# One fused GNN and transformer kernel: edge lists read before the last row tiles are turned, projections split around the counting stage, pair sums of weights formed before a move

## The chip, the cores and the metric

The kernel runs on one core of a Trainium2 chip. The metric is the device time of one execution in microseconds (us), as the median of several. The core has five engines with a queue each: TensorE (PE in the profile; its weight loads are PEld), VectorE (DVE), ScalarE (ACT), GpSimd (POOL) and SyncE (SP, which here only issues DMAs). They run beside each other and wait for each other through semaphores.

## The reference

`x` is 1250 x 768 in fp32. There are 41250 edges (`src`, `dst`), sorted by `dst`, with a loop at each node.

```
y   = layernorm(x)
h   = gat(y, W1, a_src1, a_dst1, b1);  h = relu(h)
x   = x + gat(h, W2, a_src2, a_dst2, b2)

gat(y):  h = y @ W;  e = leaky_relu((h @ a_src)[src] + (h @ a_dst)[dst])
         w = exp(e - max over the edges of a dst)
         out[dst] = sum(w * h[src]) / sum(w) + b

z   = layernorm(x)
z1  = z + attention(layernorm(z))          # 12 heads of 64, 1250 tokens
z2  = z1 + moe(layernorm(z1))              # 8 experts, the best 2 of each token
out = x + z2
```

The reference works in fp32 throughout.

## The kernel before

Nodes go in ten row tiles of 125 (T = 125, NT = 10), features in six chunks of 128 (DC = 6). An fp32 matmul shows as two passes in the profile.

**Rows and edge lists (from L219).** The edge key `dst * 1250 + src` is written to a DRAM list. For each of five blocks of two row tiles (NU = 5) an indirect DMA gathers a row of the list, `first_edges` counts with it where the block's edges begin, and a second indirect DMA gathers windows of 128 keys into `win` (L307). Meanwhile the row tiles are loaded and normalised: `spread(t)` takes mean and variance on VectorE and the root on ScalarE, `normal(t)` scales the row on ScalarE, and `columns(t)` turns the tile on PE into `xnT` (L146), with two evictions on ScalarE (L278). `project` multiplies a row tile by `gW1` (L209: 12 matmuls, 24 passes) and evicts it to `h` (L212). A `manual_schedule` block fixes the order of PE, VectorE and POOL here, as written; ScalarE's order is the planner's, except that `keep_in_program_order` puts an instruction behind the one that was written before it on its engine. The planner is the library's: it orders by its own costs the instructions whose order the text does not fix.

Behind the tiles the list entries are cleaned on VectorE (L358 to L371), a matmul `psum` (L373) counts the valid ones, `good` and `turns` (L375, L377) say whether the lists hold every edge, five transposes turn `win` into `pl` (L385) and ScalarE copies them to `lt` (L386). `lt` and `jf` lie in a pool, `onehot`, that takes the space of the row tiles.

**Counts (L399 to L412).** The counts are a 1250 x 1250 matrix of how often an edge occurs, `cnt`. In 25 groups VectorE builds a one-hot `ohp` by comparing with `lane` (L405), and for each five groups one `ohj` by comparing with `upto` (L402); both lie in `onehot` too. PE multiplies them, 25 matmuls a group (L409), and ScalarE casts the result into `cnt` (L411). `lane` and `upto` are filled by POOL's iota (L255, L337). A loop of `turns` iterations (L418), which the given lists run zero times, follows; at its end every engine waits until all that was issued before it is done. Instructions written behind it are ordered by themselves.

**First graph layer.** Loops are added to `cnt` (L438). VectorE multiplies `gW1` by the two attention vectors (`attention_vector`, L187), PE multiplies the result by `xnT` (`attention_terms`, L199, three chunks) and turns the terms to columns (L478). VectorE forms the maximum over the neighbours (L489). `rest_of_first` then projects the tiles that are left, `range(EARLY, NT)` with EARLY = 3: seven of ten. ScalarE and VectorE make the weight tiles (L517 to L522, ten for each of three parts, twelve buffers), and PE aggregates (L529). The second layer does the same with `gW2`.

**Attention (from L612).** Products of the weights run by a scheme with seven instead of eight block products (`seven`), for which POOL forms sums and differences of blocks. Of the weights: `left_sums` (L639 to L642), once for each of six pairs of heads, in `queries_keys(p)`, whose loads of `wqk` SP issues (L701). Of the rows: `t2`, `t3`. These are moved by POOL (L877, L878) into `kept`, in the space of the value weights `wv`, once PE has read `wv` for the last time. A unit is a pair of heads and a third of the queries: PE makes `scores` (L752), ScalarE copies them out of PSUM (L756; two buffers), VectorE keeps the maximum (L762) and subtracts it (L783), ScalarE takes exponentials (L784), POOL adds them up (L789, `acc`) and PE makes `values` (L797). PE's order is written out by hand in the loop over units; the products of the next pair (L684) go between.

In the code before, `queries_keys(1)` begins at the first round of that loop, behind the two moves:

```
            kept = wpool.tile([P, DC, D], F32, tag="w", name="kept")...
            ys = right(*parts(kept, NH, 2))
            nc.gpsimd.tensor_copy(ys[5], t2)
            nc.gpsimd.tensor_copy(ys[6], t3)
```

The projection, the experts and the routing behind it are not touched.

Of the kernel before, what the change touches and what calls it, by code (L numbers as in the profile page):

```python
# [27 lines left out]
def gnn_ffn_kernel(  # L28
# [137 lines left out]
    with tc.tile_pool(name="cnt", bufs=1) as cpool:  # L166
# [49 lines left out]
            nc.vector.memset(h[:, :, D:D + 1], 1.0)  # L216
            return h

        EARLY = 3  # L219
        with tc.tile_pool(name="edge", bufs=1) as ep, \  # L220
                tc.tile_pool(name="epc", bufs=2, space=PSUM) as epc, \
                tc.tile_pool(name="gpt0", bufs=2, space=PSUM) as gpt, \
# [11 lines left out]
            for i, (eng, a) in enumerate(((nc.sync, dst), (nc.scalar, src))):  # L234
# [16 lines left out]
            nc.gpsimd.iota(nodes, pattern=[[N, N]], base=0, channel_multiplier=0,  # L251
                           allow_small_or_imprecise_dtypes=True)

            lane = ep.tile([P, P, PG], BF16, name="lane")
            nc.gpsimd.iota(lane, pattern=[[1, P], [0, PG]], base=0, channel_multiplier=0,  # L255
                           allow_small_or_imprecise_dtypes=True)
            upto = ep.tile([P, 2 * NT, 5 * PG], BF16, name="upto")


# [21 lines left out]
            with tc.tile_pool(name="early", bufs=1) as xp:  # L281
# [46 lines left out]
                with tc.manual_schedule(engines=fixed):  # L328
                    pk = find_rows()
                    spread(0)  # L330
                    nc.vector.tensor_scalar(row, pk[:T, :NU], -1.0, None, ALU.add)
                    nc.vector.tensor_scalar(edges, pk[:T, :NU], -1.0, float(EC), ALU.add, ALU.mult)
                    for u in range(NU):
                        nc.gpsimd.indirect_dma_start(
                            out=krows[u], out_offset=None, in_=rows,
                            in_offset=bass.IndirectOffsetOnAxis(ap=row[:, u:u + 1], axis=0))
                    nc.gpsimd.iota(upto, pattern=[[1, 2 * NT], [0, 5 * PG]], base=1, channel_multiplier=0,  # L337
                                   allow_small_or_imprecise_dtypes=True)
                    for t in range(1, 4):
                        spread(t)  # L340
                        normal(t - 1)
                        columns(t - 1)
                    normal(3)
                    columns(3)

                    for t in range(4, NT):
                        if t < 4 + NU:
                            first_edges(t - 4)
                        spread(t)
                        if t > 4:  # L350
                            normal(t - 1)
                        if t % 2 == 0:
                            project(xT, gw, h, gpo, [t // 2 - 2])
                        if t > 4:
                            columns(t - 1)
                    normal(NT - 1)
                    columns(NT - 1)
                    nc.vector.tensor_tensor(win, win, pair[:, :, None].to_broadcast([T, NU, SL]), ALU.subtract)  # L358

            op = edge.enter_context(tc.tile_pool(name="onehot", bufs=2))  # L360
            reps = [every_partition(a, op, "rep", nc.sync) for a in (ga_src1, ga_dst1)]

            wf = win.rearrange("p u s -> p (u s)")
            ge = ep.tile([T, NU * SL], F32, name="ge")
            nc.vector.tensor_scalar(ge, wf, 0.0, None, ALU.is_ge)
            found = ep.tile([T, 1], F32, name="found")
            nc.vector.scalar_tensor_tensor(ge, wf, 2.0 * N, ge, op0=ALU.is_lt, op1=ALU.mult,
                                           accum_out=found)
            FAR = 1048576.0
            nc.vector.scalar_tensor_tensor(wf, wf, FAR, ge, op0=ALU.add, op1=ALU.mult)  # L370
            nc.vector.tensor_scalar(wf, wf, -FAR, None, ALU.add)  # L371
            pf = gpt.tile([P, 4, P], F32, tag="tr", name="psum")
            nc.tensor.matmul(pf[:, 0, 0:1], ones[:T, :P], found, start=True, stop=True)  # L373
            good = ep.tile([P, 1], F32, name="good")
            nc.vector.tensor_scalar(good, pf[:, 0, 0:1], float(E), None, ALU.is_equal)  # L375
            turns = ep.tile([1, 1], I32, name="turns")
            nc.vector.tensor_scalar(turns, good[0:1], -float(EC // EB), float(EC // EB), ALU.mult, ALU.add)  # L377


            lt = op.tile([P, NP], F32, name="lt", bufs=1)  # L380
            for u0 in range(0, NU, 4):
                n = min(4, NU - u0)
                pt = gpt.tile([P, 4, P], F32, tag="tr", name="pl")
                for u in range(u0, u0 + n):
                    nc.tensor.transpose(pt[:, u - u0, :T], win[:, u, :], ident[:T, :T])  # L385
                nc.scalar.copy(lt[:, u0 * T:(u0 + n) * T].rearrange("p (u q) -> p u q", q=T), pt[:, :n, :T])  # L386

            jf = op.tile([P, NP], F32, name="jf", bufs=1)
            half = (T - 1) // 2
            nc.vector.tensor_scalar(jf, lt, -float(half), 1.0 / T, ALU.add, ALU.mult)  # L390
            nc.vector.tensor_scalar(jf, jf, 12582912.0, -12582912.0, ALU.add, ALU.add)
# [44 lines left out]
            for t in range(NT):  # L436
                d = cnt[:, t, t * T:(t + 1) * T]
                nc.vector.tensor_tensor(d, d, ident[:T, :T], ALU.add)  # L438
            for i, a in enumerate(reps):
                attention_vector(0, i, gw, a, op, "scr")  # L440
            attention_terms(xT, gpt)
# [2 lines left out]
        with tc.tile_pool(name="gwork", bufs=2) as gp, \  # L444
# [166 lines left out]
    with tc.tile_pool(name="att", bufs=2, reuse_waits="tile") as ap, \  # L611
# [126 lines left out]
        class Unit:  # L738
# [42 lines left out]
            def weights(self, j):  # L781
                w, s = self.w, self.s[j]
                nc.vector.tensor_tensor(s[:, :, :w], s[:, :, :w], self.mb[:T, :, :w], ALU.subtract)  # L783
                nc.scalar.activation(s[:, :, :w], s[:, :, :w], AF.Exp, scale=HD ** -0.5)  # L784
                if j == 1:
                    self.acc = ap.tile([T, 2, CW], F32, tag="acc", name="acc", bufs=1)
                if 0 < j < self.ns:
                    prev = self.s[0] if j == 1 else self.acc
                    nc.gpsimd.tensor_tensor(self.acc[:, :, :w], prev[:, :, :w], s[:, :, :w], ALU.add)  # L789

            def values(self, j):
                w, s = self.w, self.s[j]
# [41 lines left out]
        with tc.tile_pool(name="tsum", bufs=1, reuse_waits="tile") as tp, \  # L834
# [42 lines left out]
            nc.gpsimd.tensor_copy(ys[5], t2)  # L877
            nc.gpsimd.tensor_copy(ys[6], t3)  # L878
        apm = ring.enter_context(tc.tile_pool(name="apm", bufs=1, space=PSUM, reuse_waits="tile"))
        apa = ring.enter_context(tc.tile_pool(name="apa", bufs=1, space=PSUM, reuse_waits="tile"))  # L880
        sx = ring.enter_context(tc.tile_pool(name="sx", bufs=1, reuse_waits="tile"))
        rings[NT:] = [sx] * (RING - NT)
        units = [(p, k) for p in range(DC) for k in range(NCK)]
        steps = last = None
        waiting = []
        for n, (p, k) in enumerate(units):
            if k == 0:
                steps = None
                if p + 1 < DC:
                    steps = queries_keys(p + 1, ys, False)  # L890
# [414 lines left out]
```

## Time and profile before

| | |
|---|---|
| median of 3 executions | 1499.6 us (1499.52 to 1505.01) |
| profiled execution | 1501.22 us |
| its span on the core | 1499.4 us |
| PE busy | 1407.0 us, 94% |
| VectorE, ScalarE, POOL busy | 813.4, 572.1, 490.1 us |
| HBM | 88 GB/s over the span |

Times in the views count from the span's start. A row of the timeline is: start, duration, engine, line, operation, output <- inputs, shape, count, and in brackets the idle time of the engine before it with what ended it. L12 is line 12 of the kernel before. In the 40 slices a digit is the busy share in tenths, and PEclk is the clock that TensorE was granted, in tenths.

### The profile page before, as it was taken

What the parts mean: (1) busy time and instruction counts of PE and PEld (TensorE: products, weight loads), DVE (VectorE), ACT (ScalarE), POOL (GpSimd) and SP (SyncE); (2) the same over time, 40 slices, a digit from 0 to 9 for tenths busy, and PEclk for the clock granted to TensorE, in tenths of its full rate; (3) what the DMA queues carried; (4) which work ended last, traced back from release to release, by engine and by line L of the source; (5) the groups of instructions that cost most, each with busy time, mean ns of one, the idle gap of its engine ahead of it and who ended that gap; (6) DMA issues with size and microseconds to landing.
All of it is one profiled execution on the core that took longest, in us unless ns stands there. A gap on an engine that the chain in (4) does not pass through costs nothing. (4 is left out here: it accounts for less than half of the span.)

```text
span 1499.4 us, 16427 instructions
## 1 busy us (share of the span) xinstructions
PE 1407.0 (94%) x6032; PEld 791.8 (53%) x6032; DVE 813.4 (54%) x1390; ACT 572.1 (38%) x920; POOL 490.1 (33%) x345
## 2 busy tenths in 40 slices
PE   5787999999999999989999999999989999899997
PEld 3584655555555556544444444444433666565654
DVE  5598545535025754356767767767767655111111
ACT  4220603205115621135656656656656223221211
POOL 5000000000000065025776867776767222222222
PEclk9757999999999999999999999999999999999999
DMA  7000020000021114990101000000001734665653
GB/s 210 22 1 11 11 74 0 1 7 26 0 87 59 52 50 157 378 363 1 33 7 28 12 8 27 13 28 7 12 19 64 238 114 146 228 227 171 225 188 121
DMA packets 55581, 128.46 MB, mean 86 GB/s; under 512 B 10797, under 2 KB 29585, under 8 KB 55498
## 3 DMA queue, kind: packets, MB, share of 16 engines
q1 hardware_dynamic: 38846, 61.18, 12.7%
q0 software_dynamic: 11968, 56.21, 10.3%
q10 hardware_dynamic: 4684, 9.99, 2.2%
q8 instruction: 48, 0.79, 0.2%
q14 instruction: 35, 0.29, 0.1%
HBM read 74.17 MB, written 57.66 MB: 88 GB/s over the span
## 5 line engine op out<-in xcount | busy, mean ns | idle before, releaser
L789 POOL TENSOR_TENSOR acc<-acc,sT 125x834 f32<-125x834 f32 (+1 forms) x139 | 273.0, 1964 | 10.7
L529 PE MATMUL pagg<-h,wt 125*125 125x385 f32 (+1 forms) x800 | 263.5, 486 | 0.4 <-DVE wt L522 0.4
L529 PEld LDWEIGHTS pagg<-h,wt 125*125 125x125 f32 x800 | 147.0, 187 | 104.6 <-DVE wt L522 3.5
L756 ACT COPY sT<-st 125x834 f32<-125x834 f32 (+1 forms) x180 | 151.3, 849 | 126.0 <-PE st L752 119.9
L783 DVE TENSOR_TENSOR sT<-sT,mb 125x834 f32<-125x834 f32 (+1 forms) x180 | 174.9, 1011 | 31.4 <-PE mb L778 31.4
L762 DVE TENSOR_TENSOR most<-most,st 125x834 f32<-125x834 f32 (+1 forms) x144 | 146.8, 1020 | 59.2 <-ACT sT L756 55.7
L784 ACT ACTIVATE sT<-sT 125x834 f32<-125x834 f32 (+1 forms) x180 | 158.4, 901 | 46.7 <-DVE sT L783 46.1
L752 PE MATMUL st<-qk 64*125 64x417 f32 (+1 forms) x720 | 163.9, 555 | 11.8 <-DVE most L762 8.3
L639 POOL TENSOR_TENSOR aT<-wv 128x1152 f32<-128x1152 f32 x1 | 2.6, 2615 | 490.0 <-DVE wt L522 490.0
L797 PE MATMUL pav<-sT,v 125*64 125x417 f32 (+1 forms) x720 | 151.0, 532 | 5.5 <-ACT sT L784 3.7
L752 PEld LDWEIGHTS st<-qk 64*125 64x125 f32 x720 | 57.0, 184 | 102.4 <-DVE most L762 51.4
L797 PEld LDWEIGHTS pav<-sT,v 125*64 125x64 f32 x720 | 42.7, 136 | 96.2 <-issue 56.1
L1039 PE MATMUL poe<-we,hT 128*128 128x384 f32 x264 | 89.8, 486 | 0.0
L1006 PE MATMUL phe<-xT,we 128*128 128x384 f32 (+1 forms) x288 | 86.6, 460 | 0.0
L1068 PE MATMUL po<-wp,aT 128*125 128x384 f32 x240 | 86.6, 497 | 0.0
L209 PE MATMUL ph<-gw,xnT 128*125 128x384 f32 x240 | 81.9, 501 | 3.4 <-DMA gw<-in_L_gnn_W_dram 3.4
L789 POOL TENSOR_TENSOR acc<-sT 125x834 f32<-125x834 f32 (+1 forms) x18 | 35.4, 1968 | 142.5 <-ACT sT L784 142.5
L533 DVE RECIPROCAL rz<-pagg 125x1 f32<-125x1 f32 x20 | 3.3, 166 | 141.0 <-PE pagg L529 141.0
L209 PE MATMUL ph<-gw,x1T 128*125 128x384 f32 x240 | 78.8, 489 | 0.0
L1008 ACT ACTIVATE hT<-phe 128x384 f32<-128x384 f32 (+2 forms) x30 | 13.1, 437 | 155.5 <-PE phe L1006 155.5
L1006 PEld LDWEIGHTS phe<-xT,we 128*128 128x128 f32 x288 | 52.1, 190 | 33.6
L1043 DVE SCALAR_TENSOR_TENSOR sofar<-poe,weight,sofar 128x768 f32<-128x768 f32 x23 | 23.4, 1018 | 82.5 <-PE poe L1039 82.5
(286 smaller groups left out, 1945.3 us busy)
## 6 DMA issues: line engine op xcount, KB each, us to landing
xd<-aT POOLq DMA_DIRECT2D x8, 3855.0 KB, 49.0
we<-in_L_ffn_W_dram SPq DMA_DIRECT2D x16, 1152.0 KB
xr<-xd SPq DMA_DIRECT2D x25, 385.5 KB
gw<-in_L_gnn_W_dram SPq DMA_DIRECT2D x2, 2304.0 KB
wqk<-in_L_ffn_Wqkv_dram SPq DMA_DIRECT2D x12, 384.0 KB
xres<-in_x_dram SPq DMA_DIRECT2D x10, 375.0 KB
xsd<-xres ACTq DMA_DIRECT2D x10, 375.0 KB
kept<-zr SPq DMA_DIRECT2D x30, 105.0 KB
```

Source lines behind the costliest of these rows:

```text
L209: nc.tensor.matmul(po[:, s, :DH], xT[:, c, t * T:(t + 1) * T], w[:, c, s * DH:(s + 1) * DH], start=(c == 0), stop=(c == DC - 1))
L529: nc.tensor.matmul(po[:, s, :DH + s], ws[j][:, (d - d0) * T:(d - d0 + 1) * T], h[:, j, s * DH:(s + 1) * DH + s], start=(j == 0), stop=(j = ...
L752: nc.tensor.matmul(st[:T, i, :w], self.qk[r, 1, j * T:(j + 1) * T], self.qk[r, 0, self.c0:self.c0 + w], start=True, stop=True)
L756: nc.scalar.copy(s[:, :, :w], st[:T, :, :w])
L762: nc.vector.tensor_tensor(self.most[:, :, :w], prev[:, :, :w], st[:T, :, :w], ALU.max)
L783: nc.vector.tensor_tensor(s[:, :, :w], s[:, :, :w], self.mb[:T, :, :w], ALU.subtract)
L784: nc.scalar.activation(s[:, :, :w], s[:, :, :w], AF.Exp, scale=HD ** -0.5)
L789: nc.gpsimd.tensor_tensor(self.acc[:, :, :w], prev[:, :, :w], s[:, :, :w], ALU.add)
L797: nc.tensor.matmul(self.pav[r, :w], v[:, j, hd0:hd0 + HD], s[:, i, :w], start=(j == 0), stop=(j == NT - 1))
L1006: nc.tensor.matmul(ph[:, :n * P], w1[:, c, f * P:(f + 1) * P], xT[:, c, :], start=(c == 0), stop=(c == DC - 1))
L1039: nc.tensor.matmul(po[:, d, :DH], hT[:, f, s * P:(s + 1) * P], w2[:, f, d * DH:(d + 1) * DH], start=(f == 0), stop=(f == FC - 1))
L1068: nc.tensor.matmul(po[:T, s, :DH], aT[:, c, t * T:(t + 1) * T], wp[:, c, s * DH:(s + 1) * DH], start=(c == 0), stop=(c == DC - 1))
```

## The change

1. `lane` and `upto` are no longer written by iotas of POOL; POOL writes 0 to 127 into a small tile, `numbers`, and ScalarE copies it, spread out, into both, behind tile 3.
2. In the fixed order tile 2 is not projected, and tiles 7 to 9 are turned last: the cleaning of the lists, `psum`, `good`, `turns` and the turning of the lists come ahead of them, and now lie in the fixed block. `lt` moves to the pool `edge`, `jf` into a part of `er`.
3. Tiles 2 and 3 are projected behind the counts and their loop, ahead of `attention_vector`. `rest_of_first` is left with six tiles.
4. `queries_keys(1)` is written ahead of the two moves, so that POOL forms the second pair's sums of weights first. The moves, and the additions of exponentials of the first unit, keep their written order on POOL.

```diff
-        EARLY = 3
+        EARLY = 2
+        MORE = 4
...
+            numbers = ep.tile([P, P], F32, name="numbers")
+            nc.gpsimd.iota(numbers, pattern=[[1, P]], base=0, channel_multiplier=0, ...)
             lane = ep.tile([P, P, PG], BF16, name="lane")
-            nc.gpsimd.iota(lane, pattern=[[1, P], [0, PG]], ...)
...
-                    nc.gpsimd.iota(upto, pattern=[[1, 2 * NT], [0, 5 * PG]], base=1, ...)
                     for t in range(1, 4):
                         spread(t)
                         normal(t - 1)
                         columns(t - 1)
                     normal(3)
                     columns(3)
+                    for o, first, n, m in ((upto, 1, 2 * NT, 5 * PG), (lane, 0, P, PG)):
+                        tc.keep_in_program_order(nc.scalar.copy(
+                            o, numbers[:, first:first + n, None].to_broadcast([P, n, m])))
 
                     for t in range(4, NT):
...
-                        if t % 2 == 0:
+                        if t in (4, 6):
                             project(xT, gw, h, gpo, [t // 2 - 2])
-                        if t > 4:
+                        if 4 < t < 8:
                             columns(t - 1)
                     normal(NT - 1)
-                    columns(NT - 1)
+                    wf = win.rearrange("p u s -> p (u s)")
+                    ge = ep.tile([T, NU * SL], F32, name="ge")
                     nc.vector.tensor_tensor(win, win, pair[:, :, None]..., ALU.subtract)
+                    ...   # L365 to L386 as they were, with lt in the pool "edge"
+                    for t in range(7, NT):
+                        columns(t)
...
-            jf = op.tile([P, NP], F32, name="jf", bufs=1)
+            jf = er[:, :NP]
...
                 nc.vector.tensor_tensor(d, d, ident[:T, :T], ALU.add)
+            project(xT, gw, h, gpo, range(EARLY, MORE))
             for i, a in enumerate(reps):
                 attention_vector(0, i, gw, a, op, "scr")
...
-                project(xT, gw, h, gpo, range(EARLY, NT))
+                project(xT, gw, h, gpo, range(MORE, NT))
...
-                    nc.gpsimd.tensor_tensor(self.acc[:, :, :w], prev[:, :, :w], s[:, :, :w], ALU.add)
+                    ins = nc.gpsimd.tensor_tensor(self.acc[:, :, :w], prev[:, :, :w], s[:, :, :w], ALU.add)
+                    if self.first == 0:
+                        tc.keep_in_program_order(ins)
...
+            ys = list(ys)
+            steps = queries_keys(1, ys, False)
+            qks.append(next(steps))
             kept = wpool.tile([P, DC, D], F32, tag="w", name="kept")...
-            ys = right(*parts(kept, NH, 2))
-            nc.gpsimd.tensor_copy(ys[5], t2)
-            nc.gpsimd.tensor_copy(ys[6], t3)
+            ys[5:] = parts(kept, NH, 2)
+            tc.keep_in_program_order(nc.gpsimd.tensor_copy(ys[5], t2))
+            tc.keep_in_program_order(nc.gpsimd.tensor_copy(ys[6], t3))
...
-        steps = last = None
+        last = None
...
-            if k == 0:
+            if k == 0 and n:
```

More of the change, by code (lines that the diff above doesn't have):

```diff
@@ L252, in gnn_ffn_kernel @@
                            allow_small_or_imprecise_dtypes=True)
+            numbers = ep.tile([P, P], F32, name="numbers")
+            nc.gpsimd.iota(numbers, pattern=[[1, P]], base=0, channel_multiplier=0,
+                           allow_small_or_imprecise_dtypes=True)
             lane = ep.tile([P, P, PG], BF16, name="lane")
-            nc.gpsimd.iota(lane, pattern=[[1, P], [0, PG]], base=0, channel_multiplier=0,
-                           allow_small_or_imprecise_dtypes=True)
             upto = ep.tile([P, 2 * NT, 5 * PG], BF16, name="upto")
@@ L336, in gnn_ffn_kernel @@
                             in_offset=bass.IndirectOffsetOnAxis(ap=row[:, u:u + 1], axis=0))
-                    nc.gpsimd.iota(upto, pattern=[[1, 2 * NT], [0, 5 * PG]], base=1, channel_multiplier=0,
-                                   allow_small_or_imprecise_dtypes=True)
                     for t in range(1, 4):
@@ L358, in gnn_ffn_kernel @@
                     nc.vector.tensor_tensor(win, win, pair[:, :, None].to_broadcast([T, NU, SL]), ALU.subtract)
+                    nc.vector.tensor_scalar(ge, wf, 0.0, None, ALU.is_ge)
+                    found = ep.tile([T, 1], F32, name="found")
+                    nc.vector.scalar_tensor_tensor(ge, wf, 2.0 * N, ge, op0=ALU.is_lt, op1=ALU.mult,
+                                                   accum_out=found)
+                    FAR = 1048576.0
+                    nc.vector.scalar_tensor_tensor(wf, wf, FAR, ge, op0=ALU.add, op1=ALU.mult)
@@ new lines, in gnn_ffn_kernel @@
+                    nc.vector.tensor_scalar(wf, wf, -FAR, None, ALU.add)
+                    ps = gpt.tile([P, 4, P], F32, tag="tr", name="psum")
+                    nc.tensor.matmul(ps[:, 0, 0:1], ones[:T, :P], found, start=True, stop=True)
+                    good = ep.tile([P, 1], F32, name="good")
+                    nc.vector.tensor_scalar(good, ps[:, 0, 0:1], float(E), None, ALU.is_equal)
+                    turns = ep.tile([1, 1], I32, name="turns")
+                    nc.vector.tensor_scalar(turns, good[0:1], -float(EC // EB), float(EC // EB), ALU.mult, ALU.add)
@@ new lines, in gnn_ffn_kernel @@
+                    lt = ep.tile([P, NP], F32, name="lt")
+                    for u0 in range(0, NU, 4):
+                        n = min(4, NU - u0)
+                        pt = gpt.tile([P, 4, P], F32, tag="tr", name="pl")
+                        for u in range(u0, u0 + n):
+                            nc.tensor.transpose(pt[:, u - u0, :T], win[:, u, :], ident[:T, :T])
+                        nc.scalar.copy(lt[:, u0 * T:(u0 + n) * T].rearrange("p (u q) -> p u q", q=T), pt[:, :n, :T])
+                    for t in range(7, NT):
+                        columns(t)
@@ L360, in gnn_ffn_kernel @@
             op = edge.enter_context(tc.tile_pool(name="onehot", bufs=2))
             reps = [every_partition(a, op, "rep", nc.sync) for a in (ga_src1, ga_dst1)]
[L363 to L386, printed above, removed]
```

## The prediction

> **What bounds the kernel now.** I read the page's slices first, to see where TensorE is not the limit.
>
> ```profile
> PE   5787999999999999989999999999989999899997
> ...
> DVE  5598545535025754356767767767767655111111
> ...
> PEclk9757999999999999999999999999999999999999
> ```
>
> A slice is 37.5 us. From the fifth slice on PE is at nine tenths at full clock; only the first four (0 to 150 us) have room, and slice 3 (75 to 112) has VectorE at nine and the granted clock at half. So whatever brings the end of that part forward, or takes a PE stall out later, moves the end of the kernel; VectorE, ScalarE and POOL work elsewhere is cover. I then took the timeline of each engine where the change works.
>
> Turning of rows and start of the counts (start, duration, engine, line; x counts passes, two per fp32 matmul):
>
> ```profile
> 22.36 11.01 PE L209 MATMUL ph<-gw,xnT 128*125 128x384 f32 x24 [3.42 <-DMA gw<-in_L_gnn_W_dram]
> ...
> 33.85 7.91 PE L209 MATMUL ph<-gw,xnT 128*125 128x384 f32 x24
> ...
> 43.78 7.91 PE L209 MATMUL ph<-gw,xnT 128*125 128x384 f32 x24
> ...
> 54.05 0.92 PE L146 MATMUL ptr<-ident,xn 125*128 125x125 f32 x6 [0.19 <-ACT xnT L278]
> 55.20 0.35 PE L373 MATMUL psum<-found,ones 125*128 125x1 f32 x2 [0.23 <-issue]
> ```
> ```profile
> 59.44 1.47 DVE L402 TENSOR_TENSOR ohj<-jb,upto 128x2500 bf16<-128x2500 bf16 x1
> ```
> ```profile
> 25.70 0.29 ACT L129 ACTIVATE sd<-mv,eps 125x1 f32<-125x1 f32 x1 [6.25 <-DVE mv L127]
> ```
>
> PE projects row tiles 0, 1 and 2 and turns all ten before it touches the edge lists, which VectorE had ready at 41.4 (L371 starts at 40.93 and takes 0.49). The counts' one-hots start at 59.44. ScalarE is idle for 6.25 us ahead of 25.70.
>
> End of the counts, up to the first aggregation (L529):
>
> ```profile
> 116.71 2.08 DVE L438 TENSOR_TENSOR cnt<-cnt,ident 125x125 uint16<-125x125 uint16 x10 [2.99 <-ACT cnt L411]
> ```
> ```profile
> 125.00 8.48 PE L199 MATMUL pe<-xnT,wa 128*32 128x417 f32 x36 [9.38 <-DVE scr L187]
> 133.41 2.34 PE L478 MATMUL pec<-four,er 128*125 128x2 f32 x20
> ```
> ```profile
> 135.62 15.08 PE L209 MATMUL ph<-gw,xnT 128*125 128x384 f32 x46
> ...
> 193.96 6.29 PE L529 MATMUL pagg<-h,wt 125*125 125x384 f32 x19
> ```
>
> PE's last count pass ends at 115.6. It then sits 9.38 us while VectorE multiplies weights by attention vectors (118.7 to 129.3), and is paced by them to 133.4. From 135.6 it is full: seven projections, then aggregations. The ten weight tiles of the first part are done at 175, so PE sets 193.6.
>
> First pair of heads, around the pair sums that POOL makes:
>
> ```profile
> 659.89 1.74 POOL L877 COPY kept<-t 128x1875 f32<-128x1875 f32 x1 [60.53 <-PE q L684]
> ...
> 670.73 1.96 POOL L789 TENSOR_TENSOR acc<-sT 125x834 f32<-125x834 f32 x1 [6.44 <-ACT sT L784]
> 672.64 0.86 POOL L640 TENSOR_TENSOR aT<-aT,wqk 128x384 f32<-128x384 f32 x1
> ```
> ```profile
> 667.66 0.97 PE L752 MATMUL st<-qk 64*125 64x417 f32 x4
> 673.56 3.50 PE L684 MATMUL pq<-kept,aT 128*128 128x313 f32 x6 [4.94 <-POOL aT L640]
> ...
> 678.54 1.67 PE L752 MATMUL st<-qk 64*125 64x417 f32 x8
> ```
> ```profile
> 674.30 1.59 ACT L756 COPY sT<-st 125x834 f32<-125x834 f32 x2
> ```
>
> POOL moves the row sums at 659.89, makes one sum, then stands at an addition of exponentials until 670.73; the next weight sum comes behind it, and PE waits 4.94 us for that. The product after the wait takes 3.50 instead of the usual 1.75.
>
> **The change, part by part.** Times are on the profiled execution: span 1499.4, 1501.2 with what lies around it, 1.6 above the median 1499.6.
>
> *Fill of `upto` and `lane`.* POOL loses two iotas (4.81 and 2.54 us), gains one of 128 elements (0.24 by the 125x125 iota). ScalarE gains copies of 2500 and 3200 elements, behind the eviction of tile 3 (18.98+0.47). No row shows such a broadcast copy. Lower bound: ScalarE's 834-element copy, 849 ns, or 1.02 ns an element: 5.8 us. Upper: the iotas that they replace, 7.4. I take 5.9. They lie in the 6.25 us of idle time; without it, the list chain has 44.4 - 41.4 = 3.0 us more before PE would notice. Cost 0. POOL's gathers may be issued about 2 us sooner, since L293 stops running beside the iota; what is late next is the loading of x and the weight, with the DMA engines full to 31 us: 0.
>
> *Tile 2's projection and tiles 7 to 9 out of the way.* Projections 0 and 1 stay where they are, to 33.85+7.91 = 41.8. The turns of tiles 5 and 6 (0.81 and 0.91 with their waits) end at 43.9 and their evictions at 44.45, as now. The `psum` matmul then runs at 44.4 instead of 55.20. From it to the one-hot is 59.44 - 55.20 = 4.24, so 48.6. Tiles 7 to 9 are turned behind it, from about 45.5, at the 1.1 us that 52.95 and 54.05 lie apart: to 48.8. `lt` and `jf` no longer lie in the row tiles' space, but the one-hot does and must wait: 49.0. Gain 10.4 (9 if VectorE's cast `rf`, 0.50, and an eviction come in between; 11 if nothing does).
>
> *The counts* run at 9.54/5 = 1.91 us per one-hot on VectorE with PE at 1.82: unchanged.
>
> *Two projections behind them.* Loop L418 makes every engine wait for the last eviction, so PE begins when L438 does: 116.71 - 10.4 = 106.3. First projection by the row at 22.36, which also begins at half clock: 11.0; the second 7.8; to 125.1. VectorE's products end at 129.3 - 10.4 = 118.9, so PE, not VectorE, is now late. The attention terms then run unpaced: the last two evictions (131.99, 133.53) lie 1.54 apart, three chunks 4.6, to 129.7; L478 2.3, to 132.0. Before, that point was 135.6: 3.6 earlier. Six projections remain instead of seven: 24 x 35.64/110 = 7.8 less. The aggregations start 3.6 + 7.8 = 11.4 earlier, at 182.2. The weight tiles move by 3.6, to 172: still 10 us of cover. Bounds: no half clock, 3.1 better; both projections wholly at half clock (0.64 a pass), 12 worse. I take the row that it resembles.
>
> Here a rule bears. The row: 24 passes in 11.01 against 7.91, 3.1 lost. The Trainium skill, "TensorE: Matmul & The Clock Gate", section "Part 1: The HAM clock gate", says that the array runs at half rate until an activity window of about 3.4 us has been busy. By that the loss is an estimated 1.7 to 3.4, and the total is 0 to 1.4 us better than mine. The trace does not bear it out in the counts:
>
> ```profile
> 78.00:81.00 3.00, 3.00 (x45) 0.50 0.03 5
> ```
>
> (length, PE busy, granted clock): a whole busy window at half clock; it stayed so from 58.5 to 130.2.
>
> *Pair sums ahead.* Four POOL additions of about 1 us pass the two moves. They need `wqk`, whose loads keep their place on SP (issued at 608.7); hardware-queue packets end before 643, so the sums fit POOL's idle 60.5 us. The moves stay at 659.89, bound by PE's last read of `wv`, and unit 0's additions stay behind them. The product can start at 668.6, not 673.56, and at 1.75: 6.7 us off that wait. But what is late next is ScalarE: values 0 and 1 end at 672.0, then scores 2 need the PSUM that the copies at 674.30 free, at 675.2, and scores 3 the maximum that VectorE reads at 676.17 to 677.19. Scores 2 and 3 now end at 680.2; then 678.2. Gain 2.0. Bounds: all ten exponentials ahead of the copies, 0.7 worse than now; copies first, the full 6.7. I take 2.0, since the ScalarE order that stands now is the nearest evidence.
>
> Sum: 11.4 + 2.0 = 13.4. The rest of the kernel is PE's and follows. Span 1486.0, execution 1487.8, median 1499.6 - 13.4 = 1486.2.
>
> **The rivals.**
> (a) *Whole stall gone.* The copies of scores come ahead of the exponentials: 4.7 more, 1481.5. For: in later units the copies do alternate with exponentials (701 to 710). Against: unit 0 has six exponentials first.
> (b) *Projections not beside VectorE's products.* The planner puts the attention terms first: they end as now less 10.4, then eight projections instead of seven: gain 10.4 - 7.8 = 2.6, plus 2.0: 1495.0. For: PE's order is not written out there. Against: the projections come first in the text and need nothing.
> (c) *The copies late.* The planner queues the two ScalarE copies in front of `lt`, on the list chain: 5.9 lost, 1492.1.
> (d) *Slower: clock stays at half.* As in the counts, the clock is not raised by the projections at 106.3. Each us at half clock costs half a us; 3.1 is in the sum, so it decides from 2 x (13.4+3.1) = 33 us of half clock on, to 139. Held up to the aggregations it costs 12 on the two projections, some 4 on the attention terms (0.90 a pass at 125, 0.51 at 132) and 6 x 7.6 on the other projections: 62 - 13.4 = 48 slower, 1548. For: the windows' row above. Against: the row at 22.36, where wide passes got fast within eleven us.
>
> That the lists do not come earlier at all would need PE's fixed order not to be kept; I see no way.
>
> **How the numbers follow.** Forecast 0.64, own range 1482 to 1490 (1.5 on the one-hot's start, 3 on the clock, 0.7 on ScalarE's order); (a) 0.16; (b) 0.09; (c) 0.06; (d) 0.05. Half a per cent, 7.5 us, is about what a measurement of this kernel tells from no change; it puts the bound at 1492.1. Forecast and (a) are faster: 0.80. (b) and (c) within: 0.15. (d) slower: 0.05. The range takes in (a), (b) and (c) and leaves (d) and the far ends: 1480 to 1495.
>
> **What would show it.** `psum` at 44.4 and the first one-hot at 49; L438 at 106; 48 passes of L209 between L438 and L199, the first ten or so at 0.64; L478 at 129.7; the first L529 at 182; L640 before 659; no wait for L640 on PE, but one of some 3 us for L756. The forecast is wrong if L199 precedes those passes, if the one-hot waits for `upto`, or if the later stages, which the planner orders anew, give back more than 3 us.

## The result and the profile after

The changed kernel takes 1490.85 us in the median (1487.07 to 1493.07), the kernel before, on the same chip, 1500.51 (1497.10 to 1505.01). The ratio is 0.9929, interval [0.9909, 0.9949]: 7.7 to 13.7 us faster, by the medians 9.7. Forecast were 13.4, which lies inside this interval: that the sum was off is read from the profiles below, not from the times. The profiled executions are 1493.07 and 1501.22 us, spans 1491.3 and 1499.4: 8.1 us apart.

The lines of after move by two to ten: `psum` is L372, `ohj` L405, the counts L412, the loops' addition L441, the column terms L482, the aggregations L533; in the attention part products are L688, scores L756, their copies L760, maxima L766, subtractions L787, exponentials L788, `values` L803.

TensorE in the graph part (start, duration, engine, line, operation, output <- inputs, shape, count, and the wait before it):

```profile
21.68 10.36 PE L209 MATMUL ph<-gw,xnT 128*125 128x384 f32 x24 [2.73 <-DMA gw<-in_L_gnn_W_dram]
...
42.83 0.35 PE L372 MATMUL psum<-found,ones 125*128 125x1 f32 x2 [0.23 <-issue]
...
106.13 18.53 PE L209 MATMUL ph<-gw,xnT 128*125 128x384 f32 x48 [2.04 <-issue]
124.59 4.39 PE L199 MATMUL pe<-xnT,wa 128*32 128x417 f32 x36
128.92 2.34 PE L482 MATMUL pec<-four,er 128*125 128x2 f32 x20
131.12 16.77 PE L209 MATMUL ph<-gw,xnT 128*125 128x384 f32 x46
...
182.91 16.31 PE L533 MATMUL pagg<-h,wt 125*125 125x384 f32 x50
```

The wait of 9.38 us behind the counts is gone: two projections, 48 passes, stand there, and the attention terms behind them take 4.39 us instead of 8.48. The aggregations start at 182.91 instead of 193.96. VectorE and ScalarE ahead of the counts:

```profile
47.90 1.47 DVE L405 TENSOR_TENSOR ohj<-jb,upto 128x2500 bf16<-128x2500 bf16 x1 [0.69 <-PE ptr L146]
```
```profile
19.35 2.28 ACT L346 CAST upto<-numbers 128x2500 bf16<-128x2500 f32 x1
21.52 2.86 ACT L346 CAST lane<-numbers 128x3200 bf16<-128x3200 f32 x1
```

The first unit of the attention: TensorE, then ScalarE, then VectorE.

```profile
656.51 1.85 PE L688 MATMUL pq<-kept,aT 128*128 128x313 f32 x6
...
665.00 1.76 PE L756 MATMUL st<-qk 64*125 64x417 f32 x4 [5.10 <-ACT sT L760]
...
668.60 3.30 PE L688 MATMUL pq<-kept,wqk 128*128 128x313 f32 x6
```
```profile
656.77 7.43 ACT L788 ACTIVATE sT<-sT 125x834 f32<-125x834 f32 x8 [3.68 <-DVE sT L787]
664.11 1.59 ACT L760 COPY sT<-st 125x834 f32<-125x834 f32 x2
```
```profile
655.72 9.43 DVE L787 TENSOR_TENSOR sT<-sT,mb 125x834 f32<-125x834 f32 x10 [1.41 <-PE mb L782]
```

The product with `aT` no longer waits for GpSimd (4.94 us before). Another wait, of 5.10 us, stands one step on, at the scores behind the first values: for ScalarE's copies, which lie behind eight exponentials. VectorE makes all ten subtractions in a row. Before, it was six and nine:

```profile
668.82 5.57 ACT L784 ACTIVATE sT<-sT 125x834 f32<-125x834 f32 x6 [3.68 <-DVE sT L783]
```
```profile
667.76 8.49 DVE L783 TENSOR_TENSOR sT<-sT,mb 125x834 f32<-125x834 f32 x9 [1.41 <-PE mb L778]
```

**How distances are read below.** Whole times of one kernel lie up to 13.4 us apart. One reason is in the profiles: the first projection starts when the weight `gw` has landed, between 19.15 and 24.43 us over the fourteen profiles of this case, whatever the edit, and all behind it moves along. So stages are compared by distances on TensorE: from the first projection to the first aggregation (*graph*: 171.59 before, 161.23 after), and from the transposes of the maxima of unit 0 to those of unit 1 (*unit 0*: 33.52 before, 35.48 after; unit 1 takes 28.22 in both).

These distances have a spread too. Seven of the profiles share the graph part of the changed kernel, and their graph distance runs from 159.41 to 161.80, since TensorE's clock is at half for a longer time in some than in others. Part of that falls on the first projection, which takes 9.69 to 11.01 us. Counted from its end, six of the seven lie between 150.5 and 151.1. In the seventh, at 148.4, the projections behind the counts took 3.1 us less. A difference of 1 to 3 us in this stage can be read only between profiles with a like clock.

### The profile page after: what moved, and what is told of

It reads as the page before. It is cut to its first block, busy times and chain, and to the rows that moved or that the text cites. A ratio compares the mean times of both kernels' runs of the same rounds, so it can differ in the third digit from the quotient of the medians.

```text
span 1491.3 us, 16427 instructions
## 1 busy us (share of the span) xinstructions
PE 1408.4 (94%) x6032; PEld 793.4 (53%) x6032; DVE 811.6 (54%) x1390; ACT 577.6 (39%) x922; POOL 483.1 (32%) x344
## 3 DMA queue, kind: packets, MB, share of 16 engines
q0 software_dynamic: 11968, 56.21, 10.4%
## 5 line engine op out<-in xcount | busy, mean ns | idle before, releaser
L533 PE MATMUL pagg<-h,wt 125*125 125x385 f32 (+1 forms) x800 | 263.5, 486 | 0.4 <-DVE wt L526 0.4
L533 PEld LDWEIGHTS pagg<-h,wt 125*125 125x125 f32 x800 | 147.0, 187 | 104.7 <-DVE wt L526 3.1
L760 ACT COPY sT<-st 125x834 f32<-125x834 f32 (+1 forms) x180 | 151.4, 849 | 125.8 <-PE st L756 120.8
L787 DVE TENSOR_TENSOR sT<-sT,mb 125x834 f32<-125x834 f32 (+1 forms) x180 | 175.0, 1012 | 31.3 <-PE mb L782 31.3
L756 PE MATMUL st<-qk 64*125 64x417 f32 (+1 forms) x720 | 165.3, 558 | 16.9 <-DVE most L766 8.1
L766 DVE TENSOR_TENSOR most<-most,st 125x834 f32<-125x834 f32 (+1 forms) x144 | 147.0, 1021 | 57.6 <-ACT sT L760 53.7
L788 ACT ACTIVATE sT<-sT 125x834 f32<-125x834 f32 (+1 forms) x180 | 158.6, 901 | 46.6 <-DVE sT L787 46.0
L803 PE MATMUL pav<-sT,v 125*64 125x417 f32 (+1 forms) x720 | 149.7, 528 | 5.9 <-ACT sT L788 4.2
L756 PEld LDWEIGHTS st<-qk 64*125 64x125 f32 x720 | 57.3, 185 | 108.0 <-DVE most L766 50.7
L803 PEld LDWEIGHTS pav<-sT,v 125*64 125x64 f32 x720 | 42.4, 135 | 95.5 <-issue 55.2
L209 PE MATMUL ph<-gw,xnT 128*125 128x384 f32 x240 | 85.8, 519 | 4.8 <-DMA gw<-in_L_gnn_W_dram 2.7
L209 PEld LDWEIGHTS ph<-gw,xnT 128*125 128x125 f32 x240 | 47.7, 202 | 39.0 <-issue 8.7
```

Of the source, the lines that this page charges most:

```text
L209: nc.tensor.matmul(po[:, s, :DH], xT[:, c, t * T:(t + 1) * T], w[:, c, s * DH:(s + 1) * DH], start=(c == 0), stop=(c == DC - 1))
L533: nc.tensor.matmul(po[:, s, :DH + s], ws[j][:, (d - d0) * T:(d - d0 + 1) * T], h[:, j, s * DH:(s + 1) * DH + s], start=(j == 0), stop=(j = ...
L756: nc.tensor.matmul(st[:T, i, :w], self.qk[r, 1, j * T:(j + 1) * T], self.qk[r, 0, self.c0:self.c0 + w], start=True, stop=True)
L760: nc.scalar.copy(s[:, :, :w], st[:T, :, :w])
L766: nc.vector.tensor_tensor(self.most[:, :, :w], prev[:, :, :w], st[:T, :, :w], ALU.max)
L803: nc.tensor.matmul(self.pav[r, :w], v[:, j, hd0:hd0 + HD], s[:, i, :w], start=(j == 0), stop=(j == NT - 1))
```

## The experiments

Three theories are named in what was expected. A is the forecast's sum. B: the pair part moved the wait to another queue and earns nothing. C: the wait is not set by what B names; the missing microseconds are half clock or a third resource.

**The graph part alone** (the attention part as before).

```diff
-            steps = queries_keys(1, ys, False)     # ahead of the moves
-            qks.append(next(steps))
...
-            if k == 0 and n:
+            if k == 0:
```

> The changed kernel with its attention part as before: only the edge lists, the copies for upto and lane, the moved tiles and projections. Theory A (the forecast's sum): the graph part is worth 11.4 us and the pair part 2.0 more, so this kernel is 11.4 us faster than before and 2 us slower than the changed one. Theory B (the pair sums moved the wait from GpSimd to ScalarE's copies and lost about 2 us of a gain of 11 to 12): this kernel is 11 to 12 us faster than before, and about 2 us faster than the changed one (1490.9 in the medians): near 1489; its lead over before is the same at the first matmul of the aggregations, at the first product of pair 1 and at the first product of unit 1, within 1 us but for half-clock stretches that fall elsewhere. Theory C (the 4 us that are missing are half-clock stretches that fall elsewhere, the pair part is worth what was forecast): its lead shrinks or grows by stretches at a granted clock near 0.5, not at the values of the first unit.

Measured: 1491.92 us, ratio 0.9945 [0.9925, 0.9965], 5.3 to 11.3 us faster than before; A gave 11.4, B 11 to 12. Graph 161.50, unit 0 33.67, with the 4.94 us wait for GpSimd as before. In the graph stage the whole gain is there; in unit 0 it is 1.8 us better than the changed kernel. The times do not tell the two apart: behind unit 1 this profile is 1.7 us longer than the changed kernel's.

**The pair part alone**, on the kernel before: the opposite edit.

```diff
+            steps = queries_keys(1, ys, False)     # ahead of the moves
+            qks.append(next(steps))
...
-            if k == 0:
+            if k == 0 and n:
```

> The kernel before with the attention part of the change alone: the sums of weights of pair 1 ahead of the move of the row sums, both in program order, the additions into acc of unit 0 in program order. Theory A (forecast): 2.0 us faster, of bounds -0.7 to 6.7; the first product with aT no longer waits for GpSimd, the next scores wait for ScalarE's copies at the time at which they were before. Theory B: ScalarE does eight exponentials ahead of the two copies instead of six, so the third and fourth scores of unit 1 start 1.5 to 2 us later than in the kernel before counted from the first product of pair 1, and the kernel is 1 to 2 us slower than before (1501 to 1502.5). Theory C: the lead at unit 1's first product is 1 to 3 us, unless a half-clock stretch falls between.

Measured: 1502.71 us, ratio 1.0014 [1.0000, 1.0027]. Unit 0 takes 34.58, 1.06 more than before; the product does not wait, the scores wait 5.09 for ScalarE. The time and the wait are theory B's, and the forecast's 2.0 us of gain lie outside the interval. But the scores do not start later, as B had it. Counted from the pair's first product they start 1.49 us earlier than before, and they and the product behind them take 6.00 us instead of 3.45, at half clock: 1.49 - 2.55 = -1.06. The moved wait alone would have left a gain; the half clock behind it turned that into a loss.

**ScalarE's order alone.**

```diff
-                nc.scalar.copy(s[:, :, :w], st[:T, :, :w])
+                ins = nc.scalar.copy(s[:, :, :w], st[:T, :, :w])
+                if self.first == NT:
+                    tc.keep_in_program_order(ins)
```
and the same for the exponentials of unit 0.

> The changed kernel with ScalarE's exponentials of unit 0 and the copies of the scores of unit 1 kept in the program's order: two exponentials, one copy, two exponentials, two copies, and so on, where the changed kernel has eight exponentials and then the copies. Theory B: the wait of 5.10 us ahead of the third scores is gone or under 1.5 us; with the half-clock stretch that follows it gone too, the first product of unit 1 is 5 to 7 us earlier than in the changed kernel; the time is 1484 to 1487. If PE then waits for VectorE or the exponentials at the values instead, 2 to 3 us are left: 1488 to 1489. Theory C (the order of ScalarE's work is not what set this stage): the wait moves to another place of the same unit with the same sum, and the time stays at 1490 to 1492.

Measured: 1491.42 us, ratio 0.9945 [0.9926, 0.9964]; unit 0 35.89. A miss for B as it stood; the time is the one that C gave, 1490 to 1492:

```profile
663.70 2.42 PE L688 MATMUL mq<-yT,aT 128*128 128x313 f32 x4 [6.93 <-DVE sT L789]
```
```profile
654.13 9.42 DVE L789 TENSOR_TENSOR sT<-sT,mb 125x834 f32<-125x834 f32 x10 [1.41 <-PE mb L784]
```

TensorE now waits for VectorE, whose ten subtractions of 0.94 us run to 663.5. A product of the next pair, which needs the bank `mb` that they read, had moved ahead of the values too. VectorE's queue stood behind ScalarE's.

**Both queues in the program's order** for unit 0.

```diff
-            with tc.manual_schedule(engines={mybir.EngineType.PE}):
+            fixed = {mybir.EngineType.PE}
+            if n == 0:
+                fixed |= {mybir.EngineType.DVE, mybir.EngineType.Activation}
+            with tc.manual_schedule(engines=fixed):
```

> The changed kernel with the work of unit 0 in the order of the program on VectorE and ScalarE too, where the changed kernel fixes TensorE alone: two subtractions, a maximum, two subtractions, two maxima, and exponentials and copies by turns, instead of ten subtractions and then the maxima. Theory B, extended by the run with ScalarE's order alone (there the wait of 5.10 us went to VectorE's ten subtractions, 9.42 us, in front of the first maximum and of the evacuation of the product): with both queues in order the stage from pair 1's first product to unit 1's first product, 35.4 us in the changed kernel, falls to 28 to 30, the sum of PE's work without the waits and without the half clock behind them; the time is 5 to 7 us under the changed kernel's, 1484 to 1486. Theory C (the order of the two queues is not what sets this stage): the wait turns up on acc, on the tiles of weights or on the bank of the scores, the stage stays above 33 us, and the time at 1490 to 1492.

Measured: 1491.60 us, ratio 0.9947 [0.9930, 0.9963]; unit 0 33.41. A miss for B again: from pair 1's first product to unit 1's it took 32.0 us, where B gave 28 to 30 and C over 33; the time is C's.

```profile
661.36 0.97 PE L756 MATMUL st<-qk 64*125 64x417 f32 x4 [0.62 <-DVE most L766]
```
```profile
660.28 2.15 DVE L766 TENSOR_TENSOR most<-most,st 125x834 f32<-125x834 f32 x2 [1.71 <-ACT sT L760]
```

No wait of TensorE is longer than 1.28 us, but there is a ring: a pair of rows is subtracted, then taken to exponentials, then the copies follow on ScalarE, and VectorE's maxima stand 1.71 us for them ahead of the next subtractions. On VectorE the pairs follow each other by 6.12 us, where TensorE needs 4.93 for one in the pipelined kernel below. Of what C named, `acc` and the tiles of weights do not show as the cause. The bank of the scores does: TensorE's scores wait 0.62 to 0.88 us for VectorE's maxima to free it. The pipelined kernel below has the same banks and no such wait, so the order makes the maxima late, not the number of banks.

**The same order without the early pair sums**: the last edit on the graph part alone.

> The graph part of the change with unit 0 in the program's order on VectorE and ScalarE, but pair 1's sums of weights behind the move of the row sums as in the kernel before. Theory B: the first product with aT waits for GpSimd as before (4.94 us, and the half clock behind it), so the stage from pair 1's first product to unit 1's first product stays at 32 to 34 us and the time at 1489 to 1492: the pair sums are worth their 5 us only where both queues are in order, and the order only where the sums are early. Rival: the queues' order was the whole matter, and GpSimd's sums come early enough once acc waits for later exponentials: stage under 31 us, 1485 to 1487.

Measured: 1489.02 us, ratio 0.9937 [0.9914, 0.9959]; unit 0 33.42, as with the early sums. The time and the stage, 32.0 us, are theory B's, but its wait for GpSimd did not come. The rival was right in that, and not in its figures, since the ring of the run before holds unit 0 here too:

```profile
649.15 0.86 POOL L644 TENSOR_TENSOR aT<-aT,wqk 128x384 f32<-128x384 f32 x1
```

GpSimd makes the sums right behind the move of the row sums, since `acc` is queued behind them and not between. So the wait before came from GpSimd's order, and the sums' place in the text is not the only way to change that.

**Unit 0 pipelined**: the same three engines fixed on the changed kernel, with `weights` split in two, `less` (the subtraction) and `power` (the exponential), and the subtractions two pairs ahead.

```diff
-                u.weights(0)
-                u.weights(1)
+                for i in range(4):      # n == 0 only
+                    u.less(i)
+                u.power(0)
+                u.power(1)
...
-                            u.weights(j + i + 2)
+                                u.power(j + i + 2)
+                    for i in range(2):
+                        if n == 0 and j + i + 4 < NT:
+                            u.less(j + i + 4)
```

> The changed kernel with unit 0's VectorE and ScalarE work in a written order that runs ahead: four subtractions first, then a maximum or two and two subtractions by turns; on ScalarE the copies of a pair of scores ahead of the next two exponentials. In the run with the plain program order (two subtractions, exponentials, copies, maxima, each pair waiting on the one before) the wait of 5.10 us was gone, but every pair of rows took 6.1 us instead of 5.1. Theory B (only this order binds unit 0): the distance from unit 0's transposes of the maxima to unit 1's, 33.5 us before and 35.5 in the changed kernel, comes down to that of the later units, 28.3, or to 30 at most, no half clock in it, and the time is 5.5 to 7 us under the changed kernel's: 1484 to 1486. Theory C (a third resource binds it, GpSimd's acc or the tiles of weights): the distance stays above 33, the time at 1490 to 1492.

Measured: 1481.92 us (1480.78 to 1483.72), ratio 0.9866 [0.9849, 0.9884]. This beats both kernels (the changed one had 0.9929 [0.9909, 0.9949]) and theory B's own 1484 to 1486. The windows (stretch, length, busy time and instructions of TensorE, its weight loads, VectorE, ScalarE and GpSimd, granted clock, share of the DMA engines, GB/s), of before, after and this kernel, from unit 0's transposes to unit 1's:

```profile
663.18:696.70 33.52, 28.54 (x128) 13.58 (x127) 21.41 (x24) 18.82 (x23) 21.29 (x14) 0.90 0.29 108
```
```profile
651.13:686.61 35.48, 30.18 (x128) 13.92 (x126) 21.60 (x24) 19.03 (x23) 17.78 (x10) 0.90 0.28 107
```
```profile
652.80:679.66 26.86, 26.81 (x128) 12.71 (x126) 21.23 (x24) 18.33 (x23) 17.85 (x10) 1.00 0.67 230
```

TensorE is busy 26.81 of 26.86 us at full clock, with the same 128 instructions. The kernel in the program's order fixes the same three engines and takes 33.41, so the order itself, and not that it is fixed, frees unit 0. The next run shows that the order held unit 0 before the change as well. VectorE now:

```profile
657.39 3.82 DVE L787 TENSOR_TENSOR sT<-sT,mb 125x834 f32<-125x834 f32 x4 [1.41 <-PE mb L782]
661.13 1.02 DVE L766 TENSOR_TENSOR most<-sT,st 125x834 f32<-125x834 f32 x1
...
662.45 1.95 DVE L787 TENSOR_TENSOR sT<-sT,mb 125x834 f32<-125x834 f32 x2
664.32 2.15 DVE L766 TENSOR_TENSOR most<-most,st 125x834 f32<-125x834 f32 x2
```

**Pipelined without the early pair sums**: that edit on the graph part alone.

> The same written order of unit 0, but pair 1's sums of weights behind the move of the row sums, as in the kernel before. Theory B, from the run with the plain order without the early sums, where GpSimd did the sums at 648 to 652, ahead of acc, and the product with aT did not wait: the distance is within 0.5 us of the run with early sums, so the pair sums are worth nothing by themselves: 1484 to 1486. Rival (they are worth their 5 us once VectorE and ScalarE are in order): the product waits 4 to 5 us again, 1489 to 1491.

Measured: 1481.69 us, ratio 0.9864 [0.9846, 0.9881]; unit 0 26.86. Once VectorE and ScalarE run in this order, the pair sums' place is worth nothing.

**No projection behind the counts.**

```diff
-        MORE = 4
+        MORE = 2
```

> The changed kernel with no projection behind the counts: all eight that are left run among the coefficients. Theory A (the forecast's step, two projections fill the 9.4 us in which PE waited for VectorE's products): PE starts the attention terms at 113 to 114 instead of 124.6, is paced by VectorE again (8.5 us instead of 4.4), and does the two projections later, at 7.8 us each: the aggregations start 8.4 us later, near 191, and the time is 1499. Rival (PE is not what bounds the coefficients and row maxima, so the two projections there are covered): the aggregations start within 3 us of 182.9, and the time is 1488 to 1494.

Measured: 1496.71 us, ratio 0.9977 [0.9961, 0.9994]; graph 169.85, 8.6 longer than in the changed kernel (8.4 expected). Theory A in the stage, though the time lies 2.3 under its 1499:

```profile
117.64 7.83 PE L199 MATMUL pe<-xnT,wa 128*32 128x417 f32 x36 [9.38 <-DVE scr L187]
```

The counts still start 8.8 us earlier than before (31.59 behind the first projection instead of 40.40), yet of that only 1.74 reach the aggregations.

**Tile 2's projection ahead again.**

```diff
-        EARLY = 2
+        EARLY = 3
...
-                        if t in (4, 6):
+                        if t in (4, 6, 8):
```

> The changed kernel with tile 2's projection ahead of the counts again: three ahead, one behind the counts, six among the coefficients. Theory A, worked out on the changed trace: psum, the one-hots and the end of the counts come 7.9 us later, PE begins behind them at 114.0, the one projection there takes 10.7, the attention terms are paced by VectorE's products again and end near 131 to 132 instead of 129: the aggregations start 2 to 3 us later, 1493 to 1494. So of the 10.4 us that the counts gain, most is only the place of one projection, and what the change earns is the gap of 9.4 us that is filled. Rival (the earlier counts earn the whole 7.9): 1498 to 1499.

Measured: 1490.91 us, ratio 0.9937 [0.9921, 0.9953]; the first count pass 36.19 behind the first projection instead of 29.60, the aggregations 160.67 instead of 161.23. Even the 2 to 3 us that were expected as a loss did not come: VectorE's products paced the terms less (one wait, 0.61). The projections behind the counts had the changed kernel's half clock here (16.77 us for the 46 passes behind the terms in both), so the clock hides no loss.

**Tiles 7 to 9 ahead of the lists again.**

```diff
-                        if 4 < t < 8:
+                        if t > 4:
                             columns(t - 1)
                     normal(NT - 1)
+                    columns(NT - 1)
...
-                    for t in range(7, NT):
-                        columns(t)
```

> The changed kernel with the transposes of row tiles 7 to 9 ahead of the edge lists again, as before; tile 2's projection stays moved. Theory A, worked out on the changed trace: psum comes 2.9 us later counted from the first projection (three tiles at 0.9 to 1.1), but ohj waited 0.69 us for those transposes in the changed kernel and no longer does, so the one-hots and all behind them come 2.2 to 2.4 us later: 1493. Rival (VectorE's or ScalarE's work on the lists is what is late): under 1 us, 1491.

Measured: 1492.34 us, ratio 0.9944 [0.9923, 0.9964]. `psum` came 2.95 us later and the first count pass 1.96 later, close to A's 2.2 to 2.4, and TensorE's wait ahead of that pass is back at 6.38 us. Yet the aggregations start 160.74 behind the first projection, no later than in the changed kernel. The clock hides a loss. The two stretches of projections behind the counts had less half clock in this profile:

```profile
105.59 17.18 PE L209 MATMUL ph<-gw,xnT 128*125 128x384 f32 x48 [2.04 <-issue]
...
129.23 15.08 PE L209 MATMUL ph<-gw,xnT 128*125 128x384 f32 x46
```

The changed kernel has 18.53 and 16.77 there, 3.0 us more. The kernel with unit 0 in the program's order, whose graph part is the changed kernel's, has 17.16 and 15.08, a like clock. Counted from the end of the first projection, its first count pass and its aggregations are both 2.3 us earlier than here. So theory A's 2.2 to 2.4 reach the aggregations, as far as one pair of profiles shows it.

**One projection behind the counts**, on the last pipelined kernel.

```diff
-        MORE = 4
+        MORE = 3
```

> The kernel with the pipelined unit 0 and without early pair sums, with one projection behind the counts instead of two, seven among the coefficients. Counted from the start of the first projection, the aggregations began at 171.6 before, 161.3 with two behind, 169.9 with none. Theory A (what earns is TensorE's idle time of 9.4 us behind the counts, no matter which work fills it): one projection at half clock takes about 10.7 and fills it, VectorE's products pace the attention terms again, the aggregations begin at 162 to 163, at most 1.5 us later than with two, and the time is 1482 to 1484. Rival (each projection moved there earns its own 7.8 us or half of the 8.6 that two earned): the aggregations begin at 165 to 166, and the time is 1486.

Measured: graph 161.19, with two behind 161.28, as theory A has it. The time, 1485.55 us, ratio 0.9897 [0.9878, 0.9916], is 3.9 us above that with two, which A does not give. The spans of the two profiles are 5.9 apart: 3.2 of it the later landing of `gw` (23.97 against 20.73), 1.4 between the aggregations and unit 0, 1.3 behind unit 1, none in the graph stage. In each of the last two stretches the clock stood at half for 3.4 us longer. Whether the other executions differ for such reasons is open.

**The iotas kept on GpSimd.**

```diff
-                    for o, first, n, m in ((upto, 1, 2 * NT, 5 * PG), (lane, 0, P, PG)):
-                        ...   # the copies
+            nc.gpsimd.iota(lane, pattern=[[1, P], [0, PG]], ...)
...
+                    nc.gpsimd.iota(upto, pattern=[[1, 2 * NT], [0, 5 * PG]], base=1, ...)
```

> The changed kernel with upto and lane filled by GpSimd as before, no copies on ScalarE. Theory A (the forecast's step: the copies lie in ScalarE's idle time, the two iotas lay in GpSimd's): no difference in the stage; the first matmul on the edge lists (psum) stays behind the second projection, 21.1 us after the first projection starts, and the time at 1490 to 1492. Rival (the iota of upto, 2.54 us on GpSimd ahead of the gathers of the lists, holds them): the gathers of the lists and psum come 1 to 2 us later, 1492 to 1493.

Measured: 1489.56 us, ratio 0.9940 [0.9916, 0.9963]; graph 160.60 against 161.23. No loss: within the spread of that stage the fill costs and earns nothing.

## Why the prediction was right, and where its sum was off

The direction, the range and the main mechanism held: 1490.85 against 1486.2, range 1480 to 1495. The range was wide enough for three of the four rivals, so the number alone confirms little. In the profiles the graph part gave 10.4 of its 11.4 us, and the pair part lost 2.0 where it was to gain 2.0.

*Fill*: 0, as forecast. The copies took 5.03 us (from 19.35 to 24.38) instead of the 5.9 estimated, inside ScalarE's idle time.

*Tile 2's projection and tiles 7 to 9 out of the way*: forecast 10.4 at the one-hots. Measured 11.5 (59.44 to 47.90), 0.7 of it the landing of `gw`; `psum` at 42.83 was forecast at 44.4. The size was right, but the text lets it look like the gain, and most of it, tile 2's share, is not. The run with tile 2's projection ahead gives back 6.6 us at the first count pass and loses nothing at the aggregations. The run with the tiles ahead gives back 2.0, and at a like clock 2.3 reach the aggregations. What earns is TensorE's idle time: between the first projection and the first aggregation the waits over half a microsecond sum to 22.4 us before and 11.9 after, 10.5 less, and the graph distance is 10.36 less. Of this 7.3 are the wait behind the counts (9.38 to 2.04), which the run with no projection there confirms (8.6 us lost). The other 3.1 are the wait ahead of the first count pass (6.48 to 3.41), which the tiles fill; with them ahead it is back at 6.38. That the two sums agree so well is partly chance: TensorE's work on the attention terms became 4.1 us shorter, and the half clock in the projections behind the counts cost 4.4 more.

*Counts*: unchanged; 52.9 us in the first profile, 52.8 in the second.

*Two projections behind them*: 18.53 us for 18.8, L441 at 105.18 for 106.3, L482 at 128.92 for 129.7. The aggregations at 182.91 for 182.2: six projections and what lies between took 51.8 us, not 50.2. Their first stretch lost 1.7 us to half clock (46 passes in 16.77 us, before 15.08), and 0.4 is a misreading: the sum started from 193.6, where the row has 193.96. On the loss behind the counts: 48 passes at 0.33 us (7.91/24) are 15.8, so 2.7 us were lost, a little under the row's 3.1; in the kernel with unit 0 in the program's order it was 1.3 (17.16). The 1.7 to 3.4 that the prediction estimated from the Trainium skill, "TensorE: Matmul & The Clock Gate", "Part 1: The HAM clock gate", hold for the first of the two and not for the second. In the counts the granted clock again stayed at 0.50 (before, from 59.2 to 130.9; the prediction read 58.5 to 130.2).

*Pair sums ahead*: this is the term that failed: forecast +2.0, bounds -0.7 to 6.7, measured -1.96 in the profile. Over the six profiles with early sums and the planner's order on VectorE and ScalarE unit 0 takes 33.93 to 35.53 us, mean 34.7; in the two with the old order 33.52 and 33.67. So it costs 0.3 to 2.0, about 1.1. Two premises fell. The copies were taken to keep their place; counted from the pair's first product they came 14.56 us after it instead of 12.70, behind eight exponentials. And the half clock was taken to go with GpSimd's wait; it came back behind the new one. Counted so, the scores started 1.49 us earlier than before, but scores and product took 6.90 us instead of 3.45. 1.49 - 3.45 = -1.96. Why the planner queued eight and not six is open, and so is why the price varies: the same wait stands before the same work in all six.

*The rest*: forecast unchanged. In the profiles the landing of `gw` gives 0.7, a half-clock stretch that before had at 345 us gives 1.0, and 1.9 are lost behind unit 1, where the clock stood at half for 20.5 us instead of 17.1. With 10.4 and -2.0 this makes, but for rounding, the 8.1 between the spans. Over all fourteen profiles the time behind unit 1 runs from 773.3 us, with 13.7 us of half clock, to 779.9, with 27.3: half a microsecond lost for each, as the prediction reckoned. This spread of 6.6 us is more than the pair sums cost. What sets the number of these stretches is open. From the aggregations to the end the changed kernel's profile gave back 2.9 us against before's, close to the 3 that the prediction named as a sign of being wrong.

*Rivals*: (a), the whole stall gone, was priced at 1481.5 us; it did not happen in the changed kernel, but the pipelined order reaches 1481.92, and unit 0 lost 6.66 us against before, the forecast's upper bound of 6.7. The copies ahead of the exponentials, as (a) had it, were not enough (35.89): VectorE's order had to go along. (b), (c) and (d) did not occur: the projections stood ahead of the terms, the copies for `lane` lay in idle time, the clock was back within the two projections.

## What to carry to other kernels

Add up the bound engine's idle time over a stage and ask which of it an edit fills: work that is only moved earlier or later on that engine, as tile 2's projection here, can leave the stage's end where it was. Compare the stretches of half clock before two profiles are read against each other: here they hid a difference of the size that was looked for. Before a wait is taken away, follow the queues of all engines that feed the next few steps, and assume that a planner's order will change with the edit; where the order binds, write it out on all of them, with the producers a step ahead, not only on the engine that waits.

## What the runs showed of the hardware

In unit 0, half clock follows a long wait. There every kernel with a TensorE wait of 4.9 to 6.9 us had a mean granted clock of 0.90 to 0.95, and every kernel whose longest wait was 1.3 us or less had 1.00. Against the 26.86 us of the pipelined kernel, a wait of about 5 us cost 1.7 to 3.6 us more than its length. The Trainium skill, "TensorE: Matmul & The Clock Gate", "Part 1: The HAM clock gate", says that an idle window of about 3.4 us throttles the array; in unit 0 the runs agree. A wait is not needed, though: in the changed kernel the granted clock was 0.50 from 132.3 to 135.7 us, and no row of TensorE from 106.13 on shows a wait ahead of that.

VectorE's maximum over a bank of scores (L766) began, where it waited, when ScalarE's copy of the same bank had ended, and the profile names the copy as what released it: 1.98 to 2.44 us of wait before, 1.71 in the program's order. Whether hardware or the order of semaphores demands that was not tried.

The landing of the first weights spread over 5.3 us (first projection at 19.15 to 24.43) between kernels that load them alike.
